# Masking attention scores: the sum and the leaky slope as one activation per graph on ScalarE, the mask as one minimum over four graphs on VectorE

## The chip, the cores and the metric

The kernel runs on one core of one Trainium2 chip. Its time is the device time of that core in microseconds (us), from the first to the last instruction and what the launch adds around them. Lower is better. A run's time is compared with other runs of the same kernel by the median.

## The reference

128 graphs of 128 nodes with 256 features pass through four residual layers. Each normalizes the features, cuts them at zero, and adds what a graph network makes of them. Layers 0 to 2 are graph attention, layer 3 is a gated graph network of three steps with a GRU cell. All of it is float32. The attention, cut to what matters (it is the same in the three layers but for a mask of nodes in layer 2, which is all ones here):

```python
h = jnp.maximum(_layernorm(x, axis=-1), 0.0)
Wh = jnp.einsum('bnf,fo->bno', h, W)
e = (Wh @ a1)[:, :, None] + (Wh @ a2)[:, None, :]
e = jnp.where(e > 0, e, 0.2 * e)                 # leaky slope
attention = jnp.where(adj > 0, e, -9e15)         # mask
attention = jax.nn.softmax(attention, axis=-1)
x = x + jax.nn.elu(jnp.einsum('bij,bjo->bio', attention, Wh))
```

In layer 3 a step is m = h @ weight[i], an aggregation over the graph's edges, and the GRU cell, h = (1 - z) n + z h.

## The kernel before, in words

**Tiling.** Nodes lie on the 128 partitions. The graphs are worked in 33 groups: the first and the last of two graphs, the 31 between of four (SIZES, L217). A group's tile of scores, em, is 128 x 512: four graphs of 128 columns. A group passes through three attention layers (`attention`, L491) and then through three GRU steps (`gru`, L736), each with two halves of the 256 features.

**One attention.** VectorE takes mean and variance (L423, L425), GpSimd the inverse root (L432, L434). ScalarE writes the normalized and cut features xn (L507), and VectorE multiplies them with the folded score vectors and sums along the row (L515): e holds for each node one number for the row part (index 0) and one for the column part (index 1). The column part has to be turned into a row that all partitions hold. The first two groups ("near") have PE transpose it into a PSUM bank, e2 (L546). All others ("far", `far = g >= FAR`) send it out to DRAM and read it back spread over the partitions, into er (L537, L539). In er the four graphs are interleaved, so that the row of one graph is read with a step of four elements (`e2_row`, L550). Then comes the part that the change touches: `masked` (L556), one VectorE instruction per graph, adds row part and column part and takes the minimum with cap; cap is +9e15 where there is an edge and -9e15 where there is none. One VectorE instruction over the group (L569) applies the slope, max(0.2 v, v). VectorE then takes the negative row maximum nmx (L571), ScalarE the exponential with the row sum (L575, one per graph), VectorE the reciprocal and the scaling (L582, L586). The weights are turned (by VectorE and DMA, L451 to L462, in the far groups; by PE, L599, in the near ones), PE gathers the features (ahp, L627), ScalarE evacuates them (ah, L634), PE multiplies with W (hp, L646), and ScalarE and VectorE form the exponential unit and the residual sum (L660, L662, L664). GpSimd prepares the residual (xo, L526).

**One GRU step.** PE aggregates over the edges (agp, L813), ScalarE copies the result (ag, L821), PE makes the gate products in five PSUM banks (nn, r, z, ni, all by L790), ScalarE evaluates the gates with tanh (L843, L848, L858, L863), VectorE combines them (L851, L856, L871 or L873, L877, L880). Attention has two PSUM banks of its own (BANKS, L235).

**Order of the work.** Nothing is issued as it is written. `plan.add` records each operation with its engine, an estimated cost in us, and a rank; `Plan.issue` (L108) then simulates the engines with these costs and sorts all operations into one order: an engine takes, of those that could start within 0.1 us of the earliest, the one of lowest rank. The rank of an attention is 3 g - lead + 2 l, with a lead of 6.5 in most groups (LEADS, L924), that of a GRU step is 3 g + i; evacuations of the GRU are ranked 2 units earlier (URGENT, L923). A load's landing is estimated from its size (`start`, L121 and following; 250 KB per us, 1.9 us, and what the load's `more` adds: 1.6 for er). Each engine executes its queue in the order thus found. A `takes` names buffers that an operation must find reserved.

Of the kernel before, what the change touches and what calls it, by code (L numbers as in the profile page):

```python
# [10 lines left out]
AF = mybir.ActivationFunctionType  # L11
OP = mybir.AluOpType
AX = mybir.AxisListType

P = 128
ALPHA = 0.2
# [23 lines left out]
class Plan:  # L40
# [21 lines left out]
    def add(self, engine, cost, rank, fn, reads=(), writes=(), after=(), takes=()):  # L62


        reads = [k if isinstance(k, tuple) else (k, None) for k in reads]
        writes = [k if isinstance(k, tuple) else (k, None) for k in writes]
        vals = list(dict.fromkeys(v for v, _ in reads + writes))
        vals += [v for v in dict.fromkeys(takes) if v not in vals]
        op = Op(engine, cost, rank, fn, vals)
        for v in vals:  # L70
            v.ops.append(op)

        def others(book, key):
            for part, ops in book.get(key[0], {}).items():
                if part is None or key[1] is None or part == key[1]:
                    yield from ops

        for key in reads:
            for d in others(self.writers, key):
                op.deps[d] = True  # L80
        for key in writes:
            for book in (self.writers, self.readers):
                for d in others(book, key):
                    op.deps.setdefault(d, False)
        for d in after:
            op.deps.setdefault(d, False)
        for v, part in writes:
            w, r = self.writers.setdefault(v, {}), self.readers.setdefault(v, {})
            if part is None:
                w.clear()  # L90
                r.clear()
            else:
                r.pop(part, None)
            w[part] = [op]
        for v, part in reads:
            if (v, part) not in writes:
                self.readers.setdefault(v, {}).setdefault(part, []).append(op)
        for d in op.deps:
            d.users.append(op)
        self.ops.append(op)  # L100
        return op
# [84 lines left out]
def kernel(  # L186
# [25 lines left out]
    nc = tc.nc  # L212
# [25 lines left out]
    add, load = plan.add, plan.load  # L238
# [4 lines left out]
    def val(pool, tag, shape, name, bufs=2, dtype=FT, cut=None):  # L243

        def make():
            if pool is None and not rw_pool:
                setup.close()
                rw_pool.append(ctx.enter_context(tc.tile_pool(name="rw", bufs=2)))
            p = rw_pool[0] if pool is None else pool
            t = p.tile([P, *shape], dtype, tag=tag, name=name, bufs=bufs)  # L250
            return t if cut is None else t[:, :cut]
        return plan.val(pool, tag, bufs, make)

    def bank(tag, name):
        n = BANKS[tag]
        return plan.val(
            psum, tag, n, lambda: psum.tile([P, T], FT, tag=tag, name=name, bufs=n)
        )
# [4 lines left out]
    def dve(cols):  # L263
        return 0.12 + cols / 1000
# [133 lines left out]
    def load_bias(dst, src):  # L398
# [8 lines left out]
        reads=[bi, bh], writes=[brz])  # L407
    add("DVE", dve(8), SETUP, lambda: nc.vector.tensor_scalar_mul(brz.t, brz.t, 0.5),
        reads=[brz], writes=[brz])
    add("DVE", dve(8), SETUP, lambda: nc.vector.tensor_scalar_mul(bh.t, bh.t, 0.5),  # L410
        reads=[bh], writes=[bh])
# [79 lines left out]
    def attention(g, l, xt, cap, xo):  # L491

        name, n = f"{g}_{l}", SIZES[g]
        rank = 3.0 * g - lead(g) + 2.0 * l
        xn = val(gw, "xn", [G, D], f"xn_{name}", cut=n)
        e = val(gw, "e", [2, G], f"e_{name}")
        far = g >= FAR
# [4 lines left out]
        if far:  # L502
            add("DVE", 0.16, rank, lambda: nc.vector.tensor_mul(nm.t, nm.t, rs.t),
                reads=[nm, rs], writes=[nm])
# [26 lines left out]
        em = val(gw, "em", [G, N], f"em_{name}", cut=n)  # L531
        if far:
# [3 lines left out]
            er = val(gw, "er", [N * G], f"er_{name}")  # L536
            load(2, rank, lambda: nc.sync.dma_start(de.t, e.t[:, 1, :n]),  # L537
                reads=[(e, (1, b)) for b in range(n)], writes=[de], takes=[er, em])
# [3 lines left out]
        else:  # L542
            e2 = bank("gat", f"e2_{name}")
# [6 lines left out]
        def e2_row(b):  # L550
            if far:
                return er.t[:, : N * n].rearrange("p (i b) -> p b i", b=n)[:, b, :]
            return e2.t[:, b * P : (b + 1) * P]


        def masked(b):  # L556
            add("DVE", dve(P) + (0.15 if far else 0.05), rank, lambda: nc.vector.scalar_tensor_tensor(  # L557
                em.t[:, b, :], e2_row(b), e.t[:, 0, b : b + 1],
                cap.t[:, b, :], op0=OP.add, op1=OP.min,
            ), reads=[er if far else (e2, b), (e, (0, b)), cap], writes=[(em, b)])  # L560

        for b in range(0 if far else n):
            row(b)
        for b in range(n):
            masked(b)
        nmx = val(gw, "nmx", [G], f"nmx_{name}", cut=n)
        sm = val(gw, "sm", [G], f"sm_{name}", cut=n)
        ri = val(gw, "ri", [G], f"ri_{name}", cut=n)
        add("DVE", dve(n * P), rank, lambda: nc.vector.scalar_tensor_tensor(  # L569
            em.t, em.t, ALPHA, em.t, op0=OP.mult, op1=OP.max), reads=[em], writes=[em])  # L570
        add("DVE", dve(n * P), rank, lambda: nc.vector.tensor_reduce(  # L571
            nmx.t, em.t, axis=AX.X, op=OP.max, negate=True), reads=[em], writes=[nmx])

# [96 lines left out]
    def gat(g):  # L670
# [16 lines left out]
        for l in range(3):  # L687
            xo = val(grp, f"x{l + 1}", [G, D], f"xo_{g}_{l}", bufs=3 if l == 2 else 2, cut=n)
            attention(g, l, xt, cap, xo)
            xt = xo  # L690
# [235 lines left out]
    def lead(g):  # L926

        return LEADS[g] if g < len(LEADS) else 6.5
# [40 lines left out]
```

## Time and profile before

| what | value |
|---|---|
| median of three runs | 2757.47 us |
| lowest and highest | 2755.29 and 2758.84 us |
| span of the profiled execution, first to last instruction | 2756.0 us |
| instructions | 32248 |
| mean granted clock of TensorE | 0.996 |
| VectorE, ScalarE, GpSimd busy | 2082.3, 1280.4, 293.7 us |

For the profiled execution the record gives the span; its time with what lies around the span is not listed apart, and the three runs lie from 0.7 below to 2.8 us above that span. In the profile PE is TensorE's matmuls and PEld its weight loads, DVE is VectorE, ACT is ScalarE, POOL is GpSimd, and SP issues the DMAs. A float32 matmul shows as two instructions. A row of the groups gives line, engine, operation, output and inputs, shapes, count, then the busy time in us and the mean ns of one, then how long the engine had stood idle just before, and what ended that. The busy time of a group counts each moment once, so where instructions overlap it is less than count times mean. A line of the waits reads: engine and line, what it waited for, us in total, times, longest.

### The profile page before, as it was taken

How to read it: one execution, taken by the hardware profiler on the slowest of the kernel's cores; microseconds unless marked ns; L12 is line 12 of the kernel's file. 1: busy time of each engine (PE TensorE's matmuls, PEld its weight loads, DVE VectorE, ACT ScalarE, POOL GpSimd, SP SyncE). 2: the span in 40 equal slices, each digit the busy share in tenths (PEclk: the TensorE clock that was granted, in tenths of full speed). 3: DMA queues.
4: the chain of work that ended last, by engine and by line, in shares of the span. 5: the costliest groups of instructions: out<-in, count | busy, mean ns of one | idle time of the engine just before them, and what ended most of it. 6: DMA issues, size and time to landing. Idle time of an engine off the chain costs nothing.

```text
span 2756.0 us, 32248 instructions
## 1 busy us (share of the span) xinstructions
PE 2712.8 (98%) x9563; PEld 1569.7 (57%) x9563; DVE 2082.3 (76%) x5541; ACT 1280.4 (46%) x2709; POOL 293.7 (11%) x369
## 2 busy tenths in 40 slices
PE   7899999999999999999999999999999999999998
PEld 4755555555555555555555555555555555555546
DVE  7778888778768887877788687778768886876643
ACT  4545444444444454444454445444444444444433
POOL 1111110101101101110111111111101010100000
PEclk9999999999999999999999999999999999999999
DMA  3113334433324433333333344323334333333310
GB/s 91 51 58 100 88 95 101 111 94 86 97 80 108 108 99 78 101 91 96 105 97 83 87 105 104 109 75 91 97 88 110 103 93 86 94 74 93 79 44 12
DMA packets 503094, 245.30 MB, mean 89 GB/s; under 512 B 280580, under 2 KB 472068, under 8 KB 502919
## 3 DMA queue, kind: packets, MB, share of 16 engines
q1 hardware_dynamic: 502918, 243.25, 33.5%
q8 instruction: 76, 1.25, 0.2%
q14 instruction: 100, 0.81, 0.1%
HBM read 139.28 MB, written 103.87 MB: 88 GB/s over the span
## 4 chain that ended last, share of the span: by engine, by line
PE 88%; DVE 8%; ACT 2%; DMA 1%; issue 1%; POOL 0%; SPq 0%; DVEq 0%; ACTq 0%; POOLq 0%
PE z L790 21%; PE r L790 21%; PE hp L646 11%; PE ni L790 11%; PE nn L790 10%; PE ahp L627 6%; PE agp L813 5%; DVE em L557 1%; DVE scr L515 1%; DVE xo L662 1%; DVE xo L664 1%; DVE d L877 1%; ACT em L575 1%; DVE h L880 1%; DVE n L856 0%
## 5 line engine op out<-in xcount | busy, mean ns | idle before, releaser
L790 PE MATMUL nn<-h,whh 128*128 128x512 f32 (+1 forms) x792 | 395.6, 581 | 1.9 <-DVE h L880 1.9
L790 PE MATMUL r<-ag,wc 128*128 128x512 f32 (+1 forms) x792 | 395.2, 581 | 1.3 <-ACT ag L821 1.3
L790 PE MATMUL ni<-ag,wc 128*128 128x512 f32 (+1 forms) x792 | 394.4, 579 | 1.4 <-ACT ag L821 1.4
L790 PE MATMUL z<-ag,wc 128*128 128x512 f32 (+1 forms) x792 | 394.2, 579 | 0.0
L790 PE MATMUL z<-h,whh 128*128 128x512 f32 (+1 forms) x792 | 394.2, 579 | 0.0
L790 PE MATMUL r<-h,whh 128*128 128x512 f32 (+1 forms) x792 | 394.2, 579 | 0.0
L851 DVE SCALAR_TENSOR_TENSOR n<-r,wn 128x512 f32<-128x512 f32 (+1 forms) x198 | 132.6, 670 | 336.5 <-ACT r L848 336.0
L646 PE MATMUL hp<-w,ah 128*128 128x256 f32 x1536 | 373.2, 381 | 0.5 <-ACT ah L634 0.2
L646 PEld LDWEIGHTS hp<-w,ah 128*128 128x128 f32 x1536 | 290.1, 190 | 131.4 <-issue 95.7
L515 DVE SCALAR_TENSOR_TENSOR scr<-xn,va 128x256 f32<-128x256 f32 x732 | 266.4, 423 | 33.9 <-ACT xn L507 33.6
L848 ACT ACTIVATE r<-r,brz 128x512 f32<-128x512 f32 (+1 forms) x198 | 133.2, 673 | 284.3 <-PE r L790 282.0
L813 PEld LDWEIGHTS agp<-am,hn 128*128 128x128 f32 x1536 | 202.3, 191 | 85.7 <-issue 73.5
L790 PEld LDWEIGHTS ni<-ag,wc 128*128 128x128 f32 x792 | 149.8, 190 | 177.9 <-issue 171.0
L790 PEld LDWEIGHTS r<-h,whh 128*128 128x128 f32 x792 | 149.3, 190 | 169.4 <-issue 162.8
L790 PEld LDWEIGHTS z<-h,whh 128*128 128x128 f32 x792 | 148.7, 190 | 168.3 <-issue 158.3
L821 ACT COPY ag<-agp 128x512 f32<-128x512 f32 (+1 forms) x198 | 113.0, 571 | 263.2 <-PE agp L813 262.8
L790 PEld LDWEIGHTS z<-ag,wc 128*128 128x128 f32 x792 | 148.4, 190 | 142.4 <-issue 138.2
L575 ACT ACTIVATE em<-em,nmx 128x128 f32<-128x128 f32 x384 | 149.4, 391 | 168.2 <-DVE nmx L571 166.4
L790 PEld LDWEIGHTS r<-ag,wc 128*128 128x128 f32 x792 | 146.1, 190 | 135.4 <-issue 120.5
L627 PEld LDWEIGHTS ahp<-at,xn 128*128 128x128 f32 x1536 | 191.3, 195 | 49.4 <-issue 37.6
L813 PE MATMUL agp<-am,hn 128*128 128x128 f32 x1536 | 205.3, 275 | 6.4 <-ACT hn L802 3.9
L526 POOL TENSOR_SCALAR xo<-xo 128x1024 f32<-128x1024 f32 (+1 forms) x66 | 73.2, 1110 | 1215.6 <-DVE xo L664 989.8
(94 smaller groups left out, 3474.1 us busy)
## 6 DMA issues: line engine op xcount, KB each, us to landing
d_hn<-tr_hn SPq DMA_DIRECT2D x116, 256.0 KB, 2.4
hn<-d_hn SPq DMA_DIRECT2D x464, 64.0 KB, 2.3
er<-de SPq DMA_DIRECT2D x90, 256.0 KB, 3.9
d_at<-tr_at SPq DMA_DIRECT2D x90, 256.0 KB, 2.0
at<-d_at SPq DMA_DIRECT2D x360, 64.0 KB, 2.0
x<-in_x_dram SPq DMA_DIRECT2D x31, 512.0 KB, 4.4
d_h<-tr_h SPq DMA_DIRECT2D x31, 512.0 KB, 2.9
h<-d_h SPq DMA_DIRECT2D x124, 128.0 KB, 3.1
```

Source lines behind the costliest of these rows:

```text
L515: add("DVE", dve(D), rank, lambda: nc.vector.scalar_tensor_tensor(scr.t, xn.t[:, b, :], 1.0 if far else rs.t[:, b : b + 1], VA[l].t[:, s, ...
L526: add("POOL", 0.14 + n * D / 1070, rank, lambda: nc.gpsimd.tensor_scalar(xo.t, xt.t, 1.0, -1.0, op0=OP.mult, op1=OP.add), reads=[xt], writ ...
L557: add("DVE", dve(P) + (0.15 if far else 0.05), rank, lambda: nc.vector.scalar_tensor_tensor(em.t[:, b, :], e2_row(b), e.t[:, 0, b : b + 1] ...
L575: add("ACT", 0.42, rank, lambda: nc.scalar.activation(em.t[:, b, :], em.t[:, b, :], AF.Exp, bias=nmx.t[:, b : b + 1], accum_out=sm.t[:, b ...
L627: add("PE", pe(P), rank, lambda: nc.tensor.matmul(summed(ps, b), xn.t[:, b, k * P : (k + 1) * P], turned_weights(b), start=True, stop=True ...
L646: add("PE", pe(D), rank, lambda: nc.tensor.matmul(hp.t[:, b * D : (b + 1) * D], ah.t[:, k, c * P : (c + 1) * P], W[l].t[:, k, :], start=(k ...
L662: add("DVE", dve(T), rank, lambda: nc.vector.scalar_tensor_tensor(u(), hp.t, 0.0, u(), op0=OP.max, op1=OP.add), reads=[hp, *parts], writes ...
L790: nc.tensor.matmul(o, w.t[:, k, c * P : (c + 1) * P], m, start=start, stop=stop)
L813: nc.tensor.matmul(ps.t[:, b * P : (b + 1) * P], s, am.t[:, b, :], start=True, stop=True)
L821: add("ACT", act(TG), quick, lambda: nc.scalar.copy(t.t[:, :TG], ps.t[:, :TG]), reads=[ps], writes=[t])
L848: add("ACT", act(TG) + 0.1, quick, lambda: nc.scalar.activation(r.t[:, :TG], pr.t[:, :TG], AF.Tanh, bias=brz.t[:, cr : cr + 1], scale=0.5) ...
L851: add("DVE", dve(TG), quick, lambda: nc.vector.scalar_tensor_tensor(n.t[:, :TG], r.t[:, :TG], 1.0, wn.t[:, :TG], op0=OP.add, op1=OP.mult), ...
```

## The change

`masked` is replaced by `sloped`. Per graph, ScalarE computes Prelu(column part + row part) in one activation: the row part is the bias per partition, the slope on the negative side is 0.2. Then one VectorE instruction over the group takes the minimum with cap, in place of the instruction that applied the slope. The mask comes after the slope instead of before it. The planner's costs go along: 0.55 us (far) or 0.42 (near) per activation on ScalarE; on VectorE the group's instruction keeps its cost, and the operation per graph is gone. The first activation reserves cap, which it doesn't read.

```diff
-        def masked(b):
-            add("DVE", dve(P) + (0.15 if far else 0.05), rank, lambda: nc.vector.scalar_tensor_tensor(
-                em.t[:, b, :], e2_row(b), e.t[:, 0, b : b + 1],
-                cap.t[:, b, :], op0=OP.add, op1=OP.min,
-            ), reads=[er if far else (e2, b), (e, (0, b)), cap], writes=[(em, b)])
+        def sloped(b):
+            add("ACT", 0.55 if far else 0.42, rank, lambda: nc.scalar.activation(
+                em.t[:, b, :], e2_row(b), AF.Prelu, bias=e.t[:, 0, b : b + 1], alpha=ALPHA,
+            ), reads=[er if far else (e2, b), (e, (0, b))], writes=[(em, b)], takes=[cap])
 
         for b in range(0 if far else n):
             row(b)
         for b in range(n):
-            masked(b)
+            sloped(b)
...
-        add("DVE", dve(n * P), rank, lambda: nc.vector.scalar_tensor_tensor(
-            em.t, em.t, ALPHA, em.t, op0=OP.mult, op1=OP.max), reads=[em], writes=[em])
+        add("DVE", dve(n * P), rank, lambda: nc.vector.tensor_tensor(
+            em.t, em.t, cap.t, op=OP.min), reads=[em, cap], writes=[em])
```

## The prediction

> **What bounds the kernel now.** I read the page from the top: the shares, the slices, then the chain of work that ended last, to find where the matrix engine (PE) is the limit and where it is not.
>
> ```profile
> PE 2712.8 (98%) x9563; PEld 1569.7 (57%) x9563; DVE 2082.3 (76%) x5541; ACT 1280.4 (46%) x2709; POOL 293.7 (11%) x369
> ...
> PE   7899999999999999999999999999999999999998
> DVE  7778888778768887877788687778768886876643
> ACT  4545444444444454444454445444444444444433
> ```
>
> PE is busy in 2712.8 of 2756.0 us, and only the first slices and the last fall short. A busy PE need not be a PE at its peak, so I check it against its own rate. The chain repeats itself every six groups:
>
> ```profile
> 1218.20 1.72 PE z L790 x4
> ...
> 1587.68 1.78 PE ahp L627 x16
> 1590.81 3.02 PE hp L646 x14
> ...
> 2086.13 1.78 PE ahp L627 x16
> 2089.25 3.02 PE hp L646 x14
> ```
>
> From 1590.81 to 2089.25 are 498.4 us, or 83.07 per group of four graphs. These rows also give the price of a matmul pass in an unbroken run: 1.72/4 = 0.430 us for 512 columns, 3.02/14 = 0.216 for 256, 1.78/16 = 0.111 for 128. A group has 144, 48 and 96 of them (gates; W products; the two kinds of gathering): 61.9 + 10.4 + 10.7 = 83.0 us. So in the middle of the run PE is at its issue rate, and all 31 full groups together hold about 31 x 0.1 = 3 us that any change could win there. By windows, PE idles 24.7 us before 100 us, 8 us from 100 to 2600, and 10.4 after. The head in ten-microsecond windows (busy PE, PEld, DVE, ACT, POOL):
>
> ```profile
> 50.00:60.00 10.00, 5.39 (x19) 3.26 (x17) 9.57 (x34) 5.01 (x14) 2.80 (x3) 0.76 0.04 8
> 60.00:70.00 10.00, 3.21 (x12) 2.47 (x11) 8.69 (x29) 2.48 (x10) 0.95 (x2) 0.67 0.06 19
> ...
> 90.00:100.00 10.00, 5.48 (x29) 4.74 (x28) 9.79 (x26) 3.95 (x13) 0.00 (x0) 0.83 0.00 0
> ```
>
> Here PE idles 4.6 + 6.8 + 4.5 = 15.9 us while VectorE is 87 to 98% busy. VectorE sets the pace in these 30 us, and nowhere later.
>
> **The rows that the change touches** (groups by line with their forms, then waits):
>
> ```profile
> L557 DVE SCALAR_TENSOR_TENSOR em<-er,e,cap 128x128 f32<-128x128 f32 x366 | 155.9, 481 | 10.4 <-DMA er<-de 10.2
> L575 ACT ACTIVATE em<-em,nmx 128x128 f32<-128x128 f32 x384 | 149.4, 391 | 168.2 <-DVE nmx L571 166.4 <-DVE ri L582 1.7
> L569 DVE SCALAR_TENSOR_TENSOR em<-em 128x512 f32<-128x512 f32 x93 | 64.7, 695 | 2.2
> L557 DVE SCALAR_TENSOR_TENSOR em<-e,e,cap 128x128 f32<-128x128 f32 x18 | 5.6, 346 | 3.7 <-PE e L546 3.4
> L507 ACT ACT_TABLE_LOAD x1 | 1.3, 1283 | 3.5 <-DMA x<-in_x_dram 3.5
> ```
>
> ```profile
> ACT em L575 <- DVE nmx L571: 166.4, 57, 5.1
> ...
> DVE em L557 <- DMA er<-de: 10.2, 13, 2.6
> PEld r L790 <- ACT ag L821: 10.0, 17, 1.0
> ```
>
> ScalarE stood idle in front of the exponential of 57 of the 99 attentions, 166.4 us in all, until VectorE had the row maximum. One instance in the timeline: it idles 4.10 us before 1130.72, while VectorE does the four mask operations (2.84 us from 1126.40), the slope and the maximum. PE lost nothing: the windows from 400 to 1800 us show it idle 1.3 us in 1400. So ScalarE may stand still for some us without PE noticing, and the stretch in which the new activations must run is one in which it mostly stood still.
>
> **What the skill says.** (1) "ScalarE: Activation LUTs", the section on what a table load costs: an activation with a bias read per partition takes about 280 ns + 0.833 ns per element, whatever the function; for 128 elements that is 387, and the exponential's row shows 391. It puts the overlap of successive ones at about 93 ns; the trace has four Relus of 587 ns in 2.08 us, a spacing of 497, so 90. (2) "ScalarE activation tables: per-element evaluation and per-set limits", section on what a function is: two functions in one set need no switch, two in different sets are one load of 1283 ns apart; the one load in this trace took 1283 ns, and it served Relu, Exp, Tanh, Identity and Copy. Neither page says in which set Prelu lies. (3) "SBUF — State Buffer", section on the two sides: a VectorE operation with two SBUF inputs and a GpSimd operation that reads SBUF exclude each other. The trace agrees: the four mask operations of 2.84 us ran beside two GpSimd operations of 1.12 and 1.07 us, against 4 x 0.43 = 1.7 us by the row's mean share.
>
> **The change part by part.**
>
> Removed: 384 mask operations on VectorE, 155.9 + 5.6 = 161.5 us busy. Replaced: 99 slope operations (64.7 + 2.5 = 67.2 us) by as many two-input minima of the same shapes. A plain two-input operation of 512 columns takes 692 ns here (the GRU's addition, L856), the slope 695: a difference of 0. VectorE: 2082 - 162 = 1921 us, 70%.
>
> Added: 384 activations of 128 columns with one per-partition bias. In a run of four they occupy 391 - 90 = 0.30 us each: 115 us. The far ones (366) read their row with a step of four elements, which no activation here does. Bounds: below, no charge, since VectorE's fastest far mask took 311 ns and its near ones 344 from PSUM; above, what separates VectorE's median far mask (438) from its fastest, 0.13 us each, or 48 us. Nothing makes a strided read a gain. I take the middle, 24 us: ScalarE 1280 + 115 + 24 = 1419 us, 51%. No engine besides PE comes near its limit.
>
> Latency of one far attention: before, 4 x 0.43 + 0.69 + 0.69 = 3.1 us on VectorE. After: 4 x 0.36 on ScalarE, a handoff to VectorE (0.06 to 0.26 us in the timeline, from the last exponential to the reciprocal; I take 0.15), then 1.4. That is 3.1 again: no change. Attention is ranked 6.5 (first layer) to 2.5 units (third) ahead of its gates, at 3 units per group of 83 us: 180 down to 69 us of cover, so neither sign matters. Without that cover 0.15 us x 93 would be 14 us.
>
> Head (likeliest -1.5 us): of the 18 near masks, 10 (3.1 us) lie at 52 to 91 us, where VectorE sets the pace, and the first far ones fall at 93. Against them stands one handoff of 0.15 us in each of four attentions. Four near masks had waited 3.4 us for PE's transposes, so their removal doesn't shorten that path. I count two thirds of 3.1 less 0.6: -1.5. Bounds: -7 (10 near and 4 far masks wholly on the path, 3.1 + 1.7, and 2 us from GpSimd's exclusion) and +3 (six handoffs and six activations that queue 0.35 us each behind setup copies).
>
> Middle (likeliest +2 us): ScalarE executes in order. Behind an activation for the scores stand the copies of aggregated messages (ag, L821), the gate activations and the evacuations of the two attention banks. Twelve activations per 83 us are 4.4 us, 5% of the time; so 5% of the 198 ag copies, 10, meet a burst. In one step of the timeline 1.8 us lie between the end of the second ag copy (2483.76) and the first product with the weights wc (2485.54); the burst is 1.5: covered, with little to spare. Today 17 copies are late, by 1.0 us at most; I add 10 late by 0.2. The planner also sorts every queue anew with the new costs (0.55 and 0.42 on ACT), SP's and PE's included; no DMA is added. The 8 us that PE idles in the middle may come out between 4 and 14: -4 to +6.
>
> Tail: the last attention ends at 2638, the gates after it are untouched: 0.
>
> Sum against the profiled span: 2756.0 - 1.5 + 2 = 2756.5. The median of the runs lies 1.5 us above that span (2757.47), which covers what lies around it: **2758.0**.
>
> **Rivals.**
> (a) ScalarE held by the row's DMA, slower. The new activation, at the head of ScalarE's queue, waits for er. VectorE waited for it 13 times, 10.2 us, 2.6 at most, arriving late because it is 76% busy; ScalarE, at 46%, would come earlier and wait more. Place: the ag copies and the two attention banks behind it. A hold decides only beyond the 1.8 us of cover: each of 2.6 us costs 0.8, so seven of them make 0.2%, and 20 of 90 make 16 us: 2774. Against it: holds of up to 5.1 us before the exponential left PE whole; the loads landed in 3.9 us by the median, and the planner reckons 256/250 + 1.9 + 1.6 = 4.5, so it places the reader late.
> (b) The head, faster: VectorE's relief passes wholly to PE there, the bound of -7: 2756.0 - 7 + 0 + 1.5 = 2750.5. For it: the 87 to 98% of VectorE beside 15.9 us of idle PE. Against: part of this stretch is a chain across all engines, in which the handoff adds.
> (c) Prelu lies in another table: two loads of 1283 ns for each of 99 attentions, 254 us on ScalarE, whose 61% would still be no bound; each pair exceeds the cover by 2.57 - 1.80 = 0.77 us: 76 us, 2834. For it: no row of this trace shows Prelu. Against: one table already serves five functions.
> (d) The change does nothing to the end, PE's rate alone deciding: 2757.5, which the forecast's case contains.
>
> **Chances.** What this measurement can tell from no change is about 0.2%, 5.5 us: below 2752.0 and above 2763.0. The forecast's case (with d) has 0.52 and its own range of 2753 to 2764, from -4 to +6; of it 0.45 are within 0.2%, 0.06 above, 0.01 below. Rival (a) 0.30: 0.26 above, 0.04 within. Rival (b) 0.14: 0.12 below, 0.02 within. Rival (c) 0.04, above. Sums: faster 0.13, same 0.51, slower 0.36. The range of 2752 to 2774 leaves out c, some 0.08 of a, and some 0.06 of b.
>
> **What would show it.** VectorE near 1920 us, ScalarE near 1420, PE's 2713 unchanged; the period of six groups still 498 us; one table load; ScalarE's idle time before the exponential down by about half, its new activations at 0.37 to 0.52 us. Rival (a) shows as long waits of ScalarE for er with PE idle right after; (b) as less than 21 us of idle PE before 100 us. I am wrong if PE idles over 15 us between 100 and 2600, or if the period of the groups moves by more than 0.2 us.

## The result, and the profile after

The changed kernel takes 2764.41 us (median of 14 runs, 2762.56 to 2767.67), the kernel before 2759.06 (median of 14 runs, 2755.29 to 2760.91). The ratio is 1.0021 with an interval of 1.0014 to 1.0029: slower by some 5 us, a shade over what was called no change. The profiles show more, 2765.9 against 2756.0 us of span. The profiled execution of the changed kernel is its longest run (2767.67, so 1.8 us lie around its span); with as much around it, that of before took some 2757.8, a little under its median. The difference between two profiles is therefore used below to find the place, and medians to say the size.

The page of the changed kernel, shares and slices:

```profile
PE 2717.0 (98%) x9563; PEld 1569.3 (57%) x9563; DVE 1948.9 (70%) x5157; ACT 1433.1 (52%) x3093; POOL 283.9 (10%) x369
...
PE   7999999999999999999999999999999999999998
...
DVE  6778777677776677776777667777676776766643
ACT  5555555455554555454554545554555554554433
```

The work moved as the diff says: VectorE lost 133 us, ScalarE gained 153, and 384 instructions changed sides. PE still has its 9563 instructions. But the chain, which repeats every four groups now, has become slower:

```profile
617.93 3.45 PE hp L645 x16
...
952.12 3.45 PE hp L645 x16
...
1286.31 3.45 PE hp L645 x16
```

That is 334.2 us for four groups, 83.55 for one, where before had 83.07. The head went the other way (same windows as in the prediction; the first number after the length is busy PE, the clock is the third from the end):

```profile
50.00:60.00 10.00, 8.57 (x37) 5.31 (x36) 9.66 (x39) 6.76 (x20) 2.61 (x3) 1.00 0.00 0
60.00:70.00 10.00, 3.58 (x17) 2.69 (x16) 7.84 (x25) 4.69 (x16) 3.80 (x5) 0.76 0.10 29
...
90.00:100.00 10.00, 9.75 (x56) 8.41 (x57) 6.76 (x16) 6.83 (x21) 0.00 (x0) 1.00 0.04 12
```

PE idled 15.9 us in these three windows before and idles 8.1 now; before 100 us it idles 19.8 us in all, where it was 24.7. The changed rows and the waits:

```profile
L557 ACT ACTIVATE em<-er,e 128x128 f32<-128x128 f32 x366 | 167.2, 519 | 13.3 <-DMA er<-de 13.1
L574 ACT ACTIVATE em<-em,nmx 128x128 f32<-128x128 f32 x384 | 149.9, 393 | 76.8 <-DVE nmx L570 73.6 <-DVE mv L425 2.4 <-ACT hn L801 0.2
L568 DVE TENSOR_TENSOR em<-em,cap 128x512 f32<-128x512 f32 x93 | 64.3, 692 | 33.4 <-ACT em L557 32.5
L557 ACT ACTIVATE em<-e,e 128x128 f32<-128x128 f32 x18 | 5.9, 368 | 6.1 <-PE e L546 4.6 <-DVE scr L515 1.4
L507 ACT ACT_TABLE_LOAD x1 | 1.3, 1283 | 3.5 <-DMA x<-in_x_dram 3.5
```

```profile
PEld agp L812 <- ACT ag L820: 24.0, 27, 1.2
PE agp L812 <- ACT ag L820: 13.7, 23, 0.9
...
ACT em L557 <- DMA er<-de: 13.1, 11, 4.5
```

The second fence holds the loss. The line PE agp <- ACT ag is not among before's waits at all, and PEld agp <- ACT ag came to 1.7 us there: PE stands in front of an aggregation until ScalarE has copied the one before it. The third line is rival (a)'s: ScalarE does wait for er, but not more often than VectorE did (13 times).

**An account of PE's time.** For every matmul pass in the trace I took the time to the start of the next one, less the price in an unbroken run (0.111, 0.216, 0.323 and 0.430 us for 128, 256, 384 and 512 columns). The sum is the time that PE lost. It is 59 us before and 69 after, and the difference is the difference of the spans. In us, by stretch:

| kernel | 0 to 100 us | 100 to 400 | 400 to 2600 | of that ahead of agp | after 2600 |
|---|---|---|---|---|---|
| before | 36.9 | 8.6 | 4.8 | 0.6 | 8.9 |
| changed | 29.8 | 11.0 | 19.4 | 18.7 | 8.9 |

The head gained 7, the middle lost 15, and all of that 15 lies in front of aggregations.

**One instance**, from the timeline of the changed kernel, with the PE and ScalarE lines of five us:

```profile
468.19 1.09 ACT L659 ACTIVATE t<-hp 128x512 f32<-128x512 f32 x2 [3.43 <-PE hp L645]
468.36 0.83 PE L812 MATMUL agp<-am,hn 128*128 128x128 f32 x6
...
469.23 0.59 ACT L820 COPY ag<-agp 128x512 f32<-128x512 f32 x1
...
469.87 1.16 PE L812 MATMUL agp<-am,hn 128*128 128x128 f32 x8 [0.68 <-ACT ag L820]
...
471.06 0.59 ACT L820 COPY ag<-agp 128x512 f32<-128x512 f32 x1 [1.25 <-PE agp L812]
...
471.70 1.16 PE L812 MATMUL agp<-am,hn 128*128 128x128 f32 x8 [0.68 <-ACT ag L820]
```

ScalarE is not late here: each copy starts within 0.04 us of the moment when the aggregation's results are there (the second one had ScalarE idle for 1.25 us). PE has nothing to do between. All aggregations write to the one PSUM bank "tr" (BANKS, L235), so two of them in a row cost the copy's 0.59 us and the handoffs, 0.68 us of idle PE. PE's queue, as sorted, says which they are:

```
agp_5_0_0 x3   (group 5, step 0, half 0; its first matmul stands 43 rows earlier)
agp_4_2_0 x4   (group 4, step 2, half 0)
agp_4_2_1 x4   (group 4, step 2, half 1)
```

In the kernel before, three gate products precede agp_4_2_0 and seven stand between it and agp_4_2_1. In the sorted queue of the changed kernel 24 pairs of different users of that bank have no PE work between them; in that of before 7. All 7 lie among the first two and the last two groups. Between 400 and 2600 us, where the groups repeat, the changed kernel has 14 such pairs and the kernel before has none. In the trace 13 of the 14 idle PE for 0.68 us and one for 0.89; by the account above, from start to start, that is 0.84 us or more each and 12 of the 18.7. Where that early first matmul comes with one gate product between it and the last user of the bank, PE loses another 0.5 us, six times; the rest is in small amounts.

### The profile page after: what moved, and what is told of

Same layout as the page of the kernel before. It is cut to its first block, busy times and chain, and to the rows that moved or that the text cites. A ratio compares the mean times of both kernels' runs of the same rounds, so it can differ in the third digit from the quotient of the medians.

```text
span 2765.9 us, 31955 instructions
## 1 busy us (share of the span) xinstructions
PE 2717.0 (98%) x9563; PEld 1569.3 (57%) x9563; DVE 1948.9 (70%) x5157; ACT 1433.1 (52%) x3093; POOL 283.9 (10%) x369
## 3 DMA queue, kind: packets, MB, share of 16 engines
q8 instruction: 76, 1.25, 0.2%
## 4 chain that ended last, share of the span: by engine, by line
PE 90%; DVE 5%; ACT 3%; DMA 1%; issue 1%; SPq 0%; POOL 0%; ACTq 0%; DVEq 0%
PE z L789 22%; PE r L789 22%; PE hp L645 11%; PE ni L789 11%; PE nn L789 11%; PE ahp L626 6%; PE agp L812 6%; ACT em L574 1%; DVE xo L663 1%; ACT hn L700 0%; DVE xo L661 0%; DVE scr L515 0%; ACT t L659 0%; ACT ag L820 0%; DVE st L423 0%
## 5 line engine op out<-in xcount | busy, mean ns | idle before, releaser
L515 DVE SCALAR_TENSOR_TENSOR scr<-xn,va 128x256 f32<-128x256 f32 x732 | 275.3, 433 | 81.9 <-ACT xn L507 80.3
L633 ACT COPY ah<-ahp 128x512 f32<-128x512 f32 (+1 forms) x198 | 112.6, 571 | 163.4 <-PE ahp L626 161.2
```

Source lines behind the costliest of these rows:

```text
L515: add("DVE", dve(D), rank, lambda: nc.vector.scalar_tensor_tensor(scr.t, xn.t[:, b, :], 1.0 if far else rs.t[:, b : b + 1], VA[l].t[:, s, ...
L633: add("ACT", act(n * P), rank, lambda: nc.scalar.copy(ah.t[:, k, : n * P], ps.t[:, : n * P]), reads=[ps], writes=[(ah, k)])
```

## The experiments

T1 is the theory that the order is what costs: the planner, given other engines and costs for 384 operations, sorted all queues anew, and the new order puts users of the bank tr next to each other. T1b, from experiment 5 on, is its narrower form: the culprit is the next group's first aggregation, taken early. T2 is the rival of the prediction: ScalarE's new work holds its queue and makes evacuations late. Each ratio is against runs of the kernel before in the same series, whose medians were 2759.85 us (experiments 1 to 4), 2758.62 (5 to 8) and 2758.41 (9 to 12).

### 1. The new instructions in the old order

```diff
-            add("ACT", 0.55 if far else 0.42, rank, lambda: nc.scalar.activation(
+            add("DVE", dve(P) + (0.15 if far else 0.05), rank, lambda: nc.scalar.activation(
...
-            ), reads=[er if far else (e2, b), (e, (0, b))], writes=[(em, b)], takes=[cap])
+            ), reads=[er if far else (e2, b), (e, (0, b)), cap], writes=[(em, b)])
...
-            em.t, em.t, cap.t, op=OP.min), reads=[em, cap], writes=[em])
+            em.t, em.t, cap.t, op=OP.min), reads=[em], writes=[em])
```

> The changed instructions (activation on ScalarE, minimum on VectorE), but the planner is told that the activation is the old VectorE operation with its old cost, so that every queue keeps the order of the kernel before. Theory T1 (the order is what costs: the new sorting puts aggregations next to each other on the one PSUM bank that they share): the stalls of the aggregations in the middle are gone again (at most 2 us of PE waiting for the ag copy instead of 13.7), and the time is that of before or lower: 2753 to 2761 us. Theory T2 (ScalarE is held by its new work, the waits for er among it, and evacuates late): the middle stays 10 to 15 us slower than before, 2765 to 2775.

Measured: 2755.90 us, ratio 0.9985 (0.9978 to 0.9992). With the order kept, the change is a gain of 4 us (2 to 6 by the interval), small beside the 5.5 us that the prediction called discernible. The row of the new activation:

```profile
L557 ACT ACTIVATE em<-er,e 128x128 f32<-128x128 f32 x366 | 166.2, 515 | 0.2 <-DMA er<-de 0.2
```

The work on ScalarE is the same 166 us; PE's lost time ahead of aggregations in the middle is 0.8 us. T2 has no room here. The head lost 35.4 us of PE time against 36.9, the middle 1.8 against 4.8.

### 2. The old instructions in the new order

```diff
-            add("DVE", dve(P) + (0.15 if far else 0.05), rank, lambda: nc.vector.scalar_tensor_tensor(
+            add("ACT", 0.55 if far else 0.42, rank, lambda: nc.vector.scalar_tensor_tensor(
...
-            ), reads=[er if far else (e2, b), (e, (0, b)), cap], writes=[(em, b)])
+            ), reads=[er if far else (e2, b), (e, (0, b))], writes=[(em, b)], takes=[cap])
...
-            em.t, em.t, ALPHA, em.t, op0=OP.mult, op1=OP.max), reads=[em], writes=[em])
+            em.t, em.t, ALPHA, em.t, op0=OP.mult, op1=OP.max), reads=[em, cap], writes=[em])
```

> The old instructions (mask on VectorE, slope on VectorE), sorted by the planner as if the mask were the new activation on ScalarE at 0.55 or 0.42 us: every queue but ScalarE's and VectorE's has the order of the changed kernel. T1: PE waits again 12 to 20 us for the ag copy in front of aggregations, 2765 to 2780 us, no faster than the changed kernel. T2: nothing is on ScalarE that wasn't there, so the waits go: 2755 to 2761.

Measured: 2816.21 us, ratio 1.0204 (1.0190 to 1.0218). PE waits 24.6 us ahead of aggregations for the ag copy, where T1 expected 12 to 20. But it is far slower than T1 said, and other waits come on top: 9.0 us of r for the ag copy and 8.0 of nn for VectorE's new state. A likely reason, not traced, is that the planner had left VectorE no time for the masks that it now does. So this run shows that the old instructions don't save the new order; the size of the loss is not the order's alone.

### 3. Another planner cost for the same instructions

```diff
-            add("ACT", 0.55 if far else 0.42, rank, lambda: nc.scalar.activation(
+            add("ACT", 0.42 if far else 0.42, rank, lambda: nc.scalar.activation(
```

> The changed kernel with one number of the planner altered: 0.42 instead of 0.55 us for the far activation. The planner then leaves PE under 2 us idle in the middle by its own reckoning (22.6 with 0.55). T1: aggregations no longer stand next to each other, PE waits under 4 us for the ag copy, and what the head gained stays: 2746 to 2756 us, faster than before. T2: ScalarE's real work is the same as in the changed kernel, so the time is too: 2762 to 2768.

Measured: 2744.81 us, ratio 0.9944 (0.9932 to 0.9957). It beats both kernels, the changed one by some 20 us, from which it differs in one number that no instruction carries. ScalarE is as busy as before:

```profile
PE 2707.8 (99%) x9563; PEld 1566.8 (57%) x9563; DVE 1936.8 (71%) x5157; ACT 1435.0 (52%) x3093; POOL 295.1 (11%) x369
```

The chain runs at 82.88 us per group (16 groups between these lines, 1326.1 us), which is PE's rate with nothing lost:

```profile
613.78 3.45 PE hp L645 x16
...
1939.85 3.45 PE hp L645 x16
```

### 4. The planner's cost as measured

```diff
-            add("ACT", 0.55 if far else 0.42, rank, lambda: nc.scalar.activation(
+            add("ACT", 0.46 if far else 0.3, rank, lambda: nc.scalar.activation(
```

> The changed kernel with the planner's costs set to what the profile measured for the activation: 0.46 us (167.2/366, far) and 0.30 (near). By its own reckoning the planner leaves PE 39 us idle in the middle. T1: more aggregations stand next to each other, PE waits 20 to 30 us for the ag copy: 2772 to 2790, although the costs are truer. T2, or the thought that a wrong cost is the fault: truer costs give an order no worse than the changed kernel's: 2755 to 2765.

Measured: 2786.35 us, ratio 1.0095 (1.0082 to 1.0109). PE lost 42 us in the middle, 30 of them ahead of aggregations and 12 ahead of nn. Truer costs made it worse. The sort doesn't respond smoothly: with 0.42 us for a far activation it is good, with 0.46 bad, with 0.55 in between (the 0.46 came with 0.30 for a near one, the others with 0.42).

### 5 and 6. The aggregations kept in turn

One rule for the planner, in the changed kernel (5) and in the kernel before (6). No instruction is added:

```diff
+    this_agg, last_agg = [], []
+
     def gru(g, xt, am, hn0, h0):
+        last_agg[:] = this_agg
+        this_agg.clear()
...
-                    add("PE", pe(P), rank + 0.1 * k, fn,
-                        reads=[hv if i > 0 else hn0, am], writes=[(ps, b)], after=after, takes=[t])
+                    op = add("PE", pe(P), rank + 0.1 * k, fn,
+                        reads=[hv if i > 0 else hn0, am], writes=[(ps, b)],
+                        after=[*after, *last_agg] if i == 0 else after, takes=[t])
+                    if i == STEPS - 1:
+                        this_agg.append(op)
```

> The changed kernel with one rule added for the planner: the first step's aggregations of a group come after the last step's aggregations of the group before. No instruction is added or altered. Theory T1b (the loss comes from the next group's first aggregation, which the new sorting slips in early and which takes the single PSUM bank that the running group's aggregations need): in the sorted order the pairs of different users of that bank with no PE work between fall from 24 to 8, PE's waits in the middle for the ag copy fall under 3 us, and the time is 2747 to 2757 us. Rival T1c (the order is bad in other ways too, and the aggregations only show it): the waits move to other products, 2760 to 2768.

Measured: 2752.83 us, ratio 0.9983 (0.9975 to 0.9990). PE's wait for the ag copy ahead of aggregations is 0.7 us in one place, its lost time in the middle 2.6 us. The rule alone turns the loss into a gain: from 1.0021 to 0.9983 is 0.38%, 10 us. T1b stands: the loss came from the next group's first aggregation, taken early into the bank that the running group needed. The rule sorts all queues anew too; experiments 6 and 8 test that it is more than a lucky sort.

> The kernel before with the same rule. There the sorting rarely slipped an aggregation in early (7 pairs with no work between, 7 with the rule too). T1b: nothing to win, 2755 to 2763 us. T1c, or the rule being good by itself: 2745 to 2752.

Measured: 2761.42 us, ratio 1.0010 (1.0003 to 1.0017). The rule has nothing to mend in the old order; it is no gain by itself.

### 7. Another planner cost for the old instructions

```diff
-            add("DVE", dve(P) + (0.15 if far else 0.05), rank, lambda: nc.vector.scalar_tensor_tensor(
+            add("DVE", dve(P) + (0.05 if far else 0.05), rank, lambda: nc.vector.scalar_tensor_tensor(
```

> The kernel before with only the planner's cost of the far mask altered, from 0.28 to 0.18 us; the instructions are the same. It asks how much of the gain of the third experiment (0.42 us for the activation) is a lucky sorting. By its own reckoning the planner's idle PE falls from 5.0 to 2.2 us in the middle and from 8.3 to 5.6 between 100 and 400 us; the head keeps its 30. If the gain is the change's: no faster than 2752 us, since the head of about 36 us stays. If it is luck: 2742 to 2748.

The expectation misstates the cost: it is 0.12 + 0.128 + 0.15 = 0.40 us, and was set to 0.30. Measured: 2761.64 us, ratio 1.0012 (1.0005 to 1.0018). An order that the planner reckoned better gave nothing, since the head lost 37.4 us as ever and the middle had little left to win (4.7 us). This sort and that of experiment 6 are no proof that none reaches 2745, but the loss in its head is what would have to go.

### 8. The measured cost and the rule together

The edits of experiments 4 and 5.

> The fourth experiment (planner's costs 0.46 and 0.30, 2786 us) with the rule of the fifth. T1b: its 30 us in front of aggregations go, and most of the 12 us in front of nn, which were waits for a state late by the same cause: 2746 to 2758 us. T1c: over 2765.

Measured: 2744.90 us, ratio 0.9953 (0.9941 to 0.9965). Experiment 4's 30 us ahead of aggregations are gone and so are its 12 us ahead of nn; the middle loses 2.3 us. ScalarE waited 10.5 us for er here (8 times), as in the changed kernel, and PE lost nothing by it.

### 9 and 10. The near groups alone, the far groups alone

Number 9 makes the change in the first two groups only, number 10 (with the edits of experiment 8) in the other 31 only:

```diff
...
         for b in range(n):
-            sloped(b)
+            (sloped if not far else masked)(b)
...
```

The fence is cut: both functions stand in the kernel, and the operation over the group is the minimum where the activation is used and the slope elsewhere. Number 10 has far in place of not far.

> The change in the first two (near) groups alone; the 31 far groups keep mask and slope on VectorE at their old costs, instruction for instruction those of before. Theory H1 (the head gains because the 18 near activations, planned on ScalarE, relieve VectorE there): PE idles 19 to 21 us before 100 us instead of 24.7. For the middle, T1 (the sorting decides) expects a loss although not one instruction there is new: the planner itself reckons 26.6 us of idle PE in the middle, and the time is 2765 to 2780 us. T2 (the ScalarE work decides) expects the middle of before, and with H1 2752 to 2757.

Measured: 2769.72 us, ratio 1.0043 (1.0031 to 1.0056). Head and middle (length, busy PE first):

```profile
0.00:100.00 100.00, 80.46 (x358) 59.19 (x359) 70.51 (x253) 54.02 (x151) 18.35 (x30) 0.95 0.24 71
100.00:2600.00 2500.00, 2479.93 (x8644) 1413.38 (x8643) 1941.22 (x5123) 1164.35 (x2464) 260.66 (x332) 1.00 0.36 93
```

PE idles 19.5 us in the head instead of 24.7, and 20 us between 100 and 2600 instead of 8, although the instructions of the far groups are those of before. A change in the first 100 us was enough to tip the sort of the other 2600. Here the lost time is mostly ahead of nn (12.3 us) and less ahead of aggregations (7.8), so the shared bank is not the only place where a bad sort costs.

> The eighth experiment (planner's cost 0.46, aggregations in turn, 2745 us) with the change in the far groups alone; the first two groups keep mask and slope on VectorE. H1: the head is that of before again, PE idles 24 to 25 us before 100 us, and the time is 4 to 7 us above the eighth's: 2749 to 2753. Against H1: the head's gain came from elsewhere, and the time stays at 2744 to 2747.

Measured: 2755.91 us, ratio 0.9992 (0.9984 to 1.0000), 11 us above experiment 8 by the two ratios, more than I expected:

```profile
0.00:100.00 100.00, 74.89 (x320) 54.77 (x321) 72.81 (x265) 48.52 (x132) 17.64 (x30) 0.88 0.24 71
100.00:2600.00 2500.00, 2493.71 (x8738) 1432.07 (x8738) 1808.47 (x4789) 1327.95 (x2845) 271.54 (x334) 1.00 0.36 93
```

The head is that of before: 25.1 us idle. Its lost time is 37.5 us against 28.9 in experiment 8, so the near groups' 18 activations, with the sort that goes with them, are worth 8.6 us, 6.0 of idle PE and the rest, by difference, in slower passes (the last section; the mean clock of the first 100 us is 0.88 here and 0.97 in experiment 8). The other 2 us lie between 100 and 400 us. I had counted only the idle part.

### 11. The dose

```diff
-        return LEADS[g] if g < len(LEADS) else 6.5
+        return LEADS[g] if g < len(LEADS) else 6.75
```

> The changed kernel with attention ranked 6.75 instead of 6.5 units ahead in most groups: the same instructions, but 113 instead of 24 pairs of different users of the one aggregation bank with no PE work between; the planner reckons 111 us of idle PE in the middle. T1: PE waits for the ag copy in front of aggregations in proportion, 70 to 110 us, 2830 to 2870 us. T2: ScalarE's work is unchanged, 2760 to 2770.

Measured: 2886.73 us, ratio 1.0472 (1.0458 to 1.0486). With 113 pairs next to each other, 101 of them between 400 and 2600 us:

```profile
PEld agp L812 <- ACT ag L820: 108.8, 110, 3.2
PE agp L812 <- ACT ag L820: 86.8, 106, 3.0
...
PE agp L812 <- DMA hn<-d_hn: 19.3, 12, 2.9
```

The wait for the ag copy has the size expected; the total is above the range, and the aggregations now wait for late states too (19.3 us). The lost time ahead of aggregations between 400 and 2600 us is 134 us with 101 pairs, against 18.7 with 14 and 0.6 with none.

### 12. The new work twice

In the kernel of experiment 3 each new activation is issued twice; the second writes the same values again.

```diff
-            add("ACT", 0.42 if far else 0.42, rank, lambda: nc.scalar.activation(
+            add("ACT", 0.42 if far else 0.42, rank, lambda: [nc.scalar.activation(
                 em.t[:, b, :], e2_row(b), AF.Prelu, bias=e.t[:, 0, b : b + 1], alpha=ALPHA,
-            ), reads=[er if far else (e2, b), (e, (0, b))], writes=[(em, b)], takes=[cap])
+            ) for _ in range(2)], reads=[er if far else (e2, b), (e, (0, b))], writes=[(em, b)], takes=[cap])
```

> The third experiment (0.42 us, 2745 us) with every new activation issued twice, one directly after the other, the second writing the same values again; the planner doesn't know, so the order stays. It adds some 384 x 0.46 = 175 us of work to ScalarE (58% busy). T1: the middle has room for it, under 5 us more: 2745 to 2750. T2 (rival a of the prediction: evacuations queue behind the activations): 2760 to 2785.

Measured: 2795.52 us, ratio 1.0133 (1.0117 to 1.0148). My expectation failed: the kernel has no such room. Against experiment 3 PE loses 7 us more in the head, 11 between 100 and 400 us and 32 in the middle. Of these 32, 13 lie ahead of the first product with ag (r<-ag), 10 ahead of nn, and none ahead of aggregations. So evacuations do come late, as T2 has it. The waits, and then one instance, from the timelines of ScalarE, VectorE and PE:

```profile
PE nn L789 <- DVE h L879: 12.6, 15, 2.7
PE r L789 <- ACT ag L820: 8.4, 12, 3.4
```

```profile
1218.59 3.99 ACT L557 ACTIVATE em<-er,e 128x128 f32<-128x128 f32 x8
...
1222.61 0.69 DVE L568 TENSOR_TENSOR em<-em,cap 128x512 f32<-128x512 f32 x1 [5.50 <-ACT em L557]
...
1237.11 1.58 ACT L507 ACTIVATE xn<-xo,nm,rs 128x256 f32<-128x256 f32 x3 [6.24 <-DVE nm L503]
1238.60 0.56 ACT L820 COPY ag<-agp 128x512 f32<-128x512 f32 x1
...
1239.21 1.13 PE L789 MATMUL r<-ag,wc 128*128 128x512 f32 x2 [0.45 <-ACT ag L820]
```

This place costs PE time 11 times, once in two groups. The copy does not stand behind the new activations. They hold VectorE, whose minimum is next in its queue and which stands idle for 5.50 us (3.28 at the same place in experiment 3). Relative to PE's work, the minimum comes 2.2 us later than there. 1.3 us of idle time on VectorE absorb part of that; its later operations, the statistics nm among them, come 0.8 us later. ScalarE has the normalizations xn ahead of the copy and stands for nm, so the copy is 0.8 us later too. In experiment 3 the copy had ended 0.24 us before PE needed it, so PE waits.

A burst directly in front of a copy did less: at 1004.40 six of the activations take 3.10 us, the copy behind them is some 0.5 us late, and PE loses nothing. After 100 us no wait of PE for an ag copy has new activations directly ahead of the copy; the longest, 3.39 us at 2474.12, has exponentials, an evacuation and normalizations there, and was not followed back, nor were the waits of nn. ScalarE at 58% was no bound by its share, and doubling the work still cost 50 us.

## Why the prediction was right and wrong

**The bound and the sums of engines: right.** PE's rate is the limit, and the best runs (experiments 3 and 8) end with 0 to 2 us lost in the middle. ScalarE came to 1433 us for 1419 predicted, nearer than the term deserved: the strided read costs a little more than the upper bound (0.457 us occupied, 519 ns each; I had taken 0.36, with bounds of 0.30 and 0.43). The two new rows hold 173 us where I had 139, but the engine's total rose by 153, as moments that overlap other instructions count once. VectorE came to 1949 for 1921; it fell by 133 and not 162, and why was not traced. There is one table load, as the forecast had it, so rival (c) is out. The idle time before the exponential fell from 166 to 74 us, "by about half".

**The head: right mechanism, wrong size.** I took -1.5 us and gave -7 as bound (rival b). Lost PE time in the head fell by 7.1, and idle PE before 100 us came to 19.8, under the 21 that was named as the sign of (b). In the old order (experiment 1) the lost time fell by 1.5, as counted; that is one profile, and the head of the old kernel in other orders lost 37.4 and 38.7 us (experiments 7 and 6), so the exact agreement is luck. The rest needs the sort to use VectorE's relief, and comes with the near groups alone (experiments 9 and 10).

**The middle: wrong.** The step that failed is the sentence "The 8 us that PE idles in the middle may come out between 4 and 14", and with it the likeliest +2. PE idles 18.7 us there, and by the prediction's own marks (over 15 us idle; a period moved by over 0.2 us, it moved by 0.48) the reasoning for this part fell. I treated the new sort as a small scatter around the old one, and looked for the loss in ScalarE's queue. It was in PE's queue: two aggregations in a row on one bank, 0.68 us of idle PE each time, while ScalarE was prompt; in all 18.7 us ahead of aggregations, of which such pairs make 12, where before had 0.6. The list of the banks, two, five and one, was in the code that I described; I named the five and the two and not the one.

**Rival (a)** had the right sign but, at this size, not the right mechanism: 13.1 us of waits for er, as before's 10.2, with 10.5 us of such waits and no PE loss from them in experiment 8. The cover of 1.8 us was read at one step and does not hold for all: in experiment 3 ScalarE stood idle for 5.44 us with an ag copy behind the xn that it waited to write, the copy still ended 0.24 us early, and in experiment 12, 0.8 us later, PE paid. Whether a wait for er alone would ever cost was not tested.

**The sum.** Predicted +0.5 us: head -1.5, middle +2. Profiled: head -7.1, 100 to 400 us +2.4, middle +14.6, end 0, together +9.9; by medians +5.4. The two errors partly cancel. That 2758.0 was near 2764.4, that the range held, and that "within 0.2%" missed only by the last digit is therefore luck and no support for the reasoning on the middle.

What stays open: why the sort tips at 0.46 and 0.55 and not at 0.42 was not traced, and only two other sorts of the old kernel were run (experiments 6 and 7), so the gain of 14 us is shown for the change with a good sort and not proved out of reach for the kernel before.

## What to carry to other kernels

When a program sorts its own queues, moving an operation between engines changes every queue; test the moved instructions in the old order first, and then the order by itself, before either is blamed. With PE at its rate, look for the resource that exists once (here a PSUM bank with one buffer) and ask whether the new order can put two of its users next to each other; a rule that keeps them in turn was worth more than a truer cost. An engine that is half idle is not free: more work on it makes the next engine wait, that one's later work comes late, and the price appears where the slack at the end of this chain is smallest, here 0.24 us before one copy. Read the slack at every such place, not at one.

## What the runs showed of the hardware

A matmul after idle time is slow, which the prediction left out of the head's price. In the kernel before, PE idles 6.79 us at 63 to 70 us, and the next gathering takes twice as long as in the middle (1.78 us for 16 passes):

```profile
70.25 1.09 PE L599 MATMUL atp<-ident,em 128*128 128x128 f32 x4 [6.79 <-DVE nm L697]
...
72.13 3.75 PE L627 MATMUL ahp<-at,xn 128*128 128x128 f32 x16 [0.29 <-DVE at L606]
```

The Trainium skill, page "TensorE: Matmul & The Clock Gate", in Part 1 on the clock gate, says that the matmul clock falls to half after an idle window of about 3.4 us and returns after as long of work. The trace agrees in part. With windows cut where the clock changes, the granted clock in the kernel before is 0.50 from 55.3 to 62.0 us, from 65.5 to 75.7 and from 96.2 to 99.6; these stretches last about two, three and one times 3.4 us. The first two begin while PE waits, and PE works for some 5 us before the second ends; the third follows a wait of 3.63 us, and the gathering in it, at 96.68, takes 3.43. But an idle window of that length is not always needed: in the changed kernel waits of 0.89 and 0.68 us, 1.8 us apart, precede a clock of 0.50 from 2144.0 to 2147.3 us.

Between 50 and 100 us the changed kernel has one such stretch, 65.2 to 72.0, and its last gathering there, at 93.36, takes 2.05 us. So idle time removed can be worth more than its length: of the 8.6 us that the near groups bring, 2.6 are not idle time, and I put them down to such passes.

A ScalarE read with a step of four elements cost 519 ns for 128 elements, against 391 for the exponential's dense one and 368 for the new activation's own dense read from PSUM.
